# An attention stage written out step by step: which steps carry no output product, where a tile's first output product is issued, and which engine makes the masks

## The chip, the cores and the metric

The kernel runs on one core of a Trainium2 chip. The metric is the device time of one execution in microseconds (us). Before the change the median of three runs is 1140.16 us (1139.94 to 1144.62). Everything is 32-bit floating point (f32) unless a type is named.

## The reference, cut to what matters

A batch of 32 sequences of 32 tokens with 512 features passes four conditional layers, each added to its input. The first three mix tokens and features with weights that are picked per sequence. The fourth, in which the change lies, is grouped-query attention over a paged cache:

```python
q = rope(rmsnorm(x @ Wq.T));  k = rope(rmsnorm(x @ Wk.T));  v = x @ Wv.T   # 32 query heads, 8 key heads, D = 128
kc, vc = k_cache[block_table], v_cache[block_table]       # 16 pages of 32 keys: 512 old keys a sequence
scores = q @ concat(kc, k).T * SCALE                      # 544 keys
scores = where(old key < cache_seqlens | new key, scores, -1e30)
o = softmax(scores) @ concat(vc, v)
x = x + o.reshape(32, 32, 32 * 128) @ Wo.T
```

The 4 query heads of a key head and the 32 tokens of a sequence make the 128 rows of one score matrix, so there are 32 x 8 = 256 score matrices of 128 x 544.

## The kernel before, in words

The first part (up to about 370 us of the profile) does the first three layers and the projections to queries, keys and values, and stores them in DRAM. The second part is the attention stage. It is one loop over steps n = 0 to 263 (`N + LAG`, N = 256, LAG = 8) under a manual schedule: every engine gets its instructions in exactly the order in which the Python code issues them, and synchronisation between engines is added by semaphores. With b, g = divmod(n, 8), step n belongs to sequence b and key head g. One step issues, in this order:

- at g = 0 to 3 one gather of cached values (`load_value_chunk`, line 252, an indirect DMA issued by GpSimd, POOL in the profile), and at several g loads of keys, queries and new values on SyncE's queue (SP);
- `scores(b, g)`: TensorE (PE) multiplies 128 queries by 288 keys (line 1019) and by 256 keys (line 1020) into the one score buffer `s_ps` in PSUM (there is only one, so the scores of the next step wait until it has been read). VectorE (DVE) reads it with one custom instruction (line 1028): it adds `mask`, scales by `rq`, writes `pr` to SBUF and gives each row's extreme in `low` by a short read-accumulator instruction;
- `exponentials`: ScalarE (ACT) takes the exponential of `pr` in place and the row sums (line 1044);
- `flip_kept`: DVE transposes finished outputs `os` into `ot` (line 1154), the step after they are made, with one exception in each four sequences;
- `fill` (n below 37 only): one of four passes of the last value projections (line 312);
- from n = 4 on, `place` for the four steps older probabilities of one quad (4 key heads): DVE transposes blocks of 32 x 32 (`turned`, line 1057), and four copies of 32 partitions x 512 put the pieces where the value product needs them (`placed`): two or three of them by ACT (line 1069), the rest by POOL (line 1071) for the first quad of a sequence (g = 4 to 7) and by DVE (line 1073) for the second (g = 0 to 3); for sequence 0 ACT takes one or two and POOL the rest of both quads. At the first step of a quad POOL gathers the new keys' probabilities (`pq`, line 1080); at the third step, which is every n with n % 4 = 2, PE transposes them (`pn_ps`, line 1084) and ACT copies the result out (line 1086);
- `share(n)`: from n = 37 on, products of the output projection. A tile is 4 sequences (128 tokens x 512 outputs), made of 32 products `f_ps` (line 1174, 128 x 512 each, accumulated in one PSUM buffer of which there is one). A tile's products are spread over 32 steps by the lists `SHARE` and `LAST` (the seventh tile, t = 6): entry i says how many products step n = 37 + 32 t + i issues. `sum` of each list is 32. After a tile's last product DVE adds it to the residual (`x`, line 1183), and that read frees the PSUM buffer. At i = 0 the sum of the tile before is also stored, by a DMA that ACT issues;
- `values` for the step eight before: PE makes four products 128 x 128 (line 1097) from `placed` and the cached values; at the fourth step of the first quad also 8 small products of the new keys (line 1117, `new_values`). At the fourth step of a quad `keep` makes DVE take the reciprocals (line 1131) and scale the output out of PSUM (`os`, line 1133);
- at g = 7 `see_keys(b + 1)`: DVE writes the next sequence's mask, 128 x 544, from a table of 16-bit key numbers and the sequence's length (line 218). There is one mask buffer, which the custom instructions of all eight steps of a sequence read.

In f32 every product is two passes on PE, so the profile counts twice as many (256 x 2 instructions for line 1019).

The lists before are `SHARE`, with entries 0 at i = 16 and i = 24 (steps with g = 5), and `LAST`, with entries 0 at i = 16, 18, 24 and 26 (g = 5, 7, 5, 7). Both have a 2 at i = 2 (g = 7) and i = 8 (g = 5). The end of the program (`finish_by_halves`) makes the eighth tile after the loop.

Of the kernel before, what the change touches and what calls it, by code (L numbers as in the profile page):

```python
# [21 lines left out]
B, S, HID = 32, 32, 512  # L22
D, HQ, HK = 128, 32, 8
# [5 lines left out]
BT = P // S  # L29
# [30 lines left out]
def cond_resid_kernel(  # L60
# [18 lines left out]
    nc = tc.nc  # L79
# [89 lines left out]
    def load_table(b: int):  # L169

        pages_of[b] = const.tile([1, NPP], I32, tag="pages", name=f"pages_{b}", bufs=4)
        at = B + b * NPP
        nc.sync.dma_start(out=pages_of[b], in_=pick[:, at : at + NPP])
# [34 lines left out]
    def load_keys(b: int):  # L208

        pool = homes[b % 2]  # L210
        kt = pool.tile([P, NPP + 1, HK * PSIZE], F32, tag="kt", name=f"kt_{b}")
        kts[b] = kt

    mask = const.tile([P, LT], F32, name="mask")

    def see_keys(b: int):

        nc.vector.tensor_scalar(
            mask, key_i, len_f[:, b : b + 1], 1.0e30, ALU.is_ge, ALU.mult
        )  # L220

    def load_new_keys(b: int):
        nc.sync.dma_start(out=kts[b][:, NPP, :], in_=k_d[b])

    def load_queries(b: int, q: int):

        qts[b, q] = qp.tile([P, HALF * S], F32, tag="qt", name=f"qt_{b}_{q}")
        nc.sync.dma_start(
            out=qts[b, q], in_=q_d[b][:, q * HALF * S : (q + 1) * HALF * S]
        )  # L230

    def load_inverses(b: int):
        rqs[b] = const.tile([P, 2, QUAD], F32, tag="rq", name=f"rq_{b}", bufs=2)
        nc.sync.dma_start(out=rqs[b], in_=r_d[:, b * S : (b + 1) * S])

    def page_keys(b: int):
        return [kts[b][:, n, :] for n in range(NPP)]
# [10 lines left out]
    def load_value_chunk(b: int, c: int):  # L248
        if c == 0:
            vts[b] = homes[b % 2].tile([P, L // P, HK * D], F32, tag="vt", name=f"vt_{b}")  # L250
        at = b * (L // P) + c
        nc.gpsimd.indirect_dma_start(  # L252
            out=vts[b][:, c, :],
            out_offset=None,
            in_=v_cache,
            in_offset=bass.IndirectOffsetOnAxis(ap=v_idx[:, at : at + 1], axis=0),
        )
# [751 lines left out]
    def quad_of(b: int, g: int):  # L1009
        return b, g // QUAD  # L1010

    def scores(b: int, g: int):
        kt, qt = kts[b], qts[quad_of(b, g)]
        kt4 = kt.rearrange("d n (h o) -> d n h o", h=HK)

        ps = ps_s.tile([P, 2 * L], F32, tag="s", name=f"s_ps_{b}_{g}")
        u = g % QUAD
        q = qt[:, u * REP * S : (u + 1) * REP * S]
        nc.tensor.matmul(ps[:, first:L], q, kt4[:, :N_LOW, g, :], start=True, stop=True)  # L1019
        nc.tensor.matmul(  # L1020
            ps[:, L : first + LT], q, kt4[:, N_LOW:, g, :], start=True, stop=True
        )
        if u == 0:
            prs[quad_of(b, g)] = tp.tile([P, QUAD, LT], F32, tag="pr", name=f"pr_{b}_{g}")
        pr = prs[quad_of(b, g)][:, u, :]
        low = tp.tile([P, 1], F32, tag="low", name=f"low_{b}_{g}", bufs=4)

        nc.vector.tensor_tensor_reduce(  # L1028
            pr,
            ps[:, first : first + LT],  # L1030
            mask,
            rqs[b][:, g // QUAD, u : u + 1],
            3.0e38,
            ALU.add,
            ALU.min,
            low,
        )
        return b, g, pr, low

    def exponentials(b: int, g: int, pr, low):  # L1040
        quad, u = quad_of(b, g), g % QUAD
        if u == 0:
            dens[quad] = tp.tile([P, QUAD], F32, tag="den", name=f"den_{b}_{g}", bufs=4)
        nc.scalar.activation(  # L1044
            pr, pr, AF.Exp, bias=low, scale=-1.0, accum_out=dens[quad][:, u : u + 1]
        )
# [114 lines left out]
    def load_residual(t: int):  # L1161
        x3s[t] = tp.tile([P, HID], F32, tag="os", name=f"x3_{t}")
        nc.sync.dma_start(out=x3s[t], in_=x_d[t])

    def finish(t: int, hs):

        for h in hs:
            if h == 0:

                if t < NT - 1:  # L1170
                    pfs[t] = ps_p.tile([P, HID], F32, tag="f", name=f"f_ps_{t}")
                else:
                    pfs[t] = ps_s.tile([P, 2 * L], F32, tag="s", name=f"f_ps_{t}")
            nc.tensor.matmul(  # L1174
                pfs[t][:, :HID],
                ots[t, h // HALF][:, h % HALF, :],
                wo(h),
                start=(h == 0),
                stop=(h == (HQ if t < NT - 1 else HALF) - 1),
            )  # L1180
            if h == HQ - 1:
                x3 = x3s.pop(t)
                nc.vector.tensor_tensor(x3, x3, pfs.pop(t), ALU.add)
                added[t] = x3
# [15 lines left out]
    def store_sum(t: int, eng):  # L1200
        eng.dma_start(out=out[t * P : (t + 1) * P, :], in_=added.pop(t))
# [2 lines left out]

    SHARE = [1, 1, 2, 1, 1, 1, 1, 1, 2, 1, 1, 1, 1, 1] + [1, 1, 0] + [1] * 7 + [0] + [1] * 7

    LAST = SHARE[:14] + [1, 1, 0, 1, 0, 1, 1, 1, 1, 1, 0, 1, 0] + [1, 1, 1, 2, 2]
    BEGIN = BT * HK + LAG - QUAD + 1  # L1210

    def share(n: int):
        t, i = divmod(n - BEGIN, BT * HK)
        if 0 <= t < NT - 1:
            parts = LAST if t == NT - 2 else SHARE
            done = sum(parts[:i])
            finish(t, range(done, done + parts[i]))
        if i == 0 and 0 < t:
            store_sum(t - 1, nc.scalar)

    units = [(b, g) for b in range(B) for g in range(HK)]
    N = len(units)
# [24 lines left out]
    with tc.manual_schedule(engines=order):  # L1247
        for n in range(N + LAG):
            b, g = divmod(n, HK)
            if n == FILLED + 2:  # L1250
                pa.close()
                late = ctx.enter_context(tc.tile_pool(name="b_w", bufs=1))
                places.append(late)
                wos[1] = late.tile([P, LATE, HID], F32, name="wo_1")
            if BEGIN <= n <= N and n % (BT * HK) == 0:

                load_residual((n - BEGIN) // (BT * HK))
            if n < N:
                if g == 0 and b >= 1:
                    load_queries(b, 1)  # L1260
                if g == 0 and 1 <= b < B - 1:
                    load_keys(b + 1)
                    load_new_keys(b + 1)
                    keys.dsts = page_keys(b + 1)
                    keys.transfer(slice(0, 12))
                if g < L // P and b >= 2:
                    load_value_chunk(b, g)
                if g == QUAD and b < B - 1:
                    load_queries(b + 1, 0)
                    load_inverses(b + 1)  # L1270
                    if b >= 1:
                        keys.transfer(slice(12, NPP))
                    if 1 <= b < B - 2:
                        load_table(b + 2)
                if g == QUAD + 1 and b >= 1:
                    load_new_values(b)
                if g == QUAD + 2 and b < B - 2:
                    keys = Picked(nc.sync, k_cache, pages_of.pop(b + 2), range(NPP), K_SHAPE)
                scored = scores(b, g)
                exponentials(*scored)  # L1280
            flip_kept(n)
            fill(n)
            if n in unstored:
                store_values(*unstored.pop(n))
            if n == QUAD + 1:
                load_new_values(0)
            if n in WO_AT:
                load_wo(2 * WO_AT.index(n))
            if QUAD <= n < N + QUAD:
                bq, i = divmod(n - QUAD, HK)  # L1290
                q, j = divmod(i, QUAD)
                if j == 0:
                    gather_new(bq, q)
                if j == 2:
                    flip_new(bq, q)
                place(bq, q, j)
            share(n)
            if n >= LAG:
                values(*units[n - LAG])
            if n < N and g == HK - 1 and b < B - 1:  # L1300
                see_keys(b + 1)
            if n > N + QUAD:
                at = 4 * (n - N - QUAD - 1)
                finish(NT - 1, range(at, at + 4))
        assert not dens and not prs and not pos and not placed and not pns
        load_residual(NT - 1)
        flip_kept(N + LAG)
        finish(NT - 1, range(3 * QUAD, HALF))
        finish_by_halves(NT - 1)
# [76 lines left out]
```

## Time and profile before

| | us |
|---|---|
| median of 3 runs | 1140.16 |
| the profiled execution's own time | 1139.8 |
| its span, first to last instruction | 1138.0 |
| PE busy | 1122.4 (99%) |
| DVE busy | 807.5 (71%) |
| ACT busy | 752.8 (66%) |
| POOL busy | 559.0 (49%) |
| masks of line 218, 32 instructions | 20.5 (DVE) |
| output products of line 1174, 480 passes | 241.3 (PE) |
| additions of line 1183, 7 instructions | 4.6 (DVE) |

"Busy" adds the durations of an engine's instructions without overlap. For PE the ends are modelled, so that a pass that had to wait for its weights looks like a longer pass; a stall is therefore read from the distance between the starts of two passes, and from PEld, the loading of weights, which shows what it waited for. In a timeline each line is: start, duration, engine, line and operation, written tile <- read tiles, shape, count, and in brackets the idle time just before and what ended it. The share of the granted TensorE clock was full over the whole span.

### The profile page before, as it was taken

What the parts mean: (1) busy time and instruction counts of PE and PEld (TensorE: products, weight loads), DVE (VectorE), ACT (ScalarE), POOL (GpSimd) and SP (SyncE); (2) the same over time, 40 slices, a digit from 0 to 9 for tenths busy, and PEclk for the clock granted to TensorE, in tenths of its full rate; (3) what the DMA queues carried; (4) which work ended last, traced back from release to release, by engine and by line L of the source; (5) the groups of instructions that cost most, each with busy time, mean ns of one, the idle gap of its engine ahead of it and who ended that gap; (6) DMA issues with size and microseconds to landing.
All of it is one profiled execution on the core that took longest, in us unless ns stands there. A gap on an engine that the chain in (4) does not pass through costs nothing. (4 is left out here: it accounts for less than half of the span.)

```text
span 1138.0 us, 18994 instructions
## 1 busy us (share of the span) xinstructions
PE 1122.4 (99%) x5432; PEld 730.1 (64%) x5432; DVE 807.5 (71%) x1670; ACT 752.8 (66%) x1900; POOL 559.0 (49%) x719
## 2 busy tenths in 40 slices
PE   8999999999999999999999999999999999999998
PEld 5554444444444577777777777777777777777766
DVE  2510688886977487777778868877877777877851
ACT  1211377576666688777777777877777877777750
POOL 3411689899897544533443344334533443344310
PEclk9999999999999999999999999999999999999999
DMA  8998447688786587888667756765776676766610
GB/s 319 392 419 347 176 133 220 174 234 229 197 232 169 159 272 267 271 308 284 216 217 243 248 190 230 262 229 178 243 251 223 200 239 224 240 202 214 222 29 10
DMA packets 173354, 259.24 MB, mean 228 GB/s; under 512 B 31522, under 2 KB 130466, under 8 KB 168770
## 3 DMA queue, kind: packets, MB, share of 16 engines
q1 hardware_dynamic: 152226, 184.22, 51.0%
q0 software_dynamic: 20016, 71.97, 17.7%
q10 hardware_dynamic: 1008, 1.84, 0.4%
q8 instruction: 44, 0.72, 0.3%
q14 instruction: 60, 0.49, 0.1%
HBM read 228.46 MB, written 37.88 MB: 234 GB/s over the span
## 5 line engine op out<-in xcount | busy, mean ns | idle before, releaser
L1069 ACT COPY placed<-turned 32x512 f32<-32x512 f32 x539 | 332.8, 617 | 31.4 <-DVE turned L1057 24.0
L1097 PEld LDWEIGHTS o_ps<-vt,placed 128*128 128x128 f32 x2048 | 267.0, 191 | 118.5 <-issue 89.4
L1028 DVE CUSTOM_DVE_ANT_0 pr<-s_ps,mask,rq 128x544 f32<-128x544 f32 x256 | 200.6, 784 | 132.5 <-PE s_ps L1020 124.0
L1044 ACT ACTIVATE pr<-pr,low 128x544 f32<-128x544 f32 x256 | 192.2, 751 | 132.7 <-DVE low L1028 130.8
L1071 POOL COPY placed<-turned 32x512 f32<-32x512 f32 x268 | 163.6, 611 | 230.8 <-DVE turned L1057 164.1
L1097 PE MATMUL o_ps<-vt,placed 128*128 128x128 f32 x2048 | 270.4, 275 | 5.6 <-ACT placed L1069 2.8
L1174 PE MATMUL f_ps<-wo,ot 128*128 128x512 f32 x480 | 241.3, 594 | 0.7
L1057 DVE STREAM_TRANSPOSE turned<-pr 128x512 f32<-128x512 f32 x256 | 178.7, 698 | 0.1
L1019 PE MATMUL s_ps<-kt,qt 128*128 128x288 f32 x512 | 174.4, 422 | 1.4 <-DVE low L1028 0.5
L1020 PE MATMUL s_ps<-kt,qt 128*128 128x256 f32 x512 | 152.3, 379 | 0.4 <-issue 0.4
L252 POOL DMA_INDIRECT vt<-in_v_cache_dram,v_idx x128 | 128.0, 1000 | 36.6 <-issue 25.4
L1020 PEld LDWEIGHTS s_ps<-kt,qt 128*128 128x128 f32 x512 | 97.2, 190 | 27.5 <-DMA kt<-in_k_cache_dram 0.8
L434 POOL TENSOR_TENSOR ra<-ra,rs 128x512 f32<-128x512 f32 x80 | 103.9, 1306 | 10.6 <-DVE rs L429 6.4
L1174 PEld LDWEIGHTS f_ps<-wo,ot 128*128 128x128 f32 x480 | 85.8, 190 | 28.6 <-issue 13.9
L1073 DVE COPY placed<-turned 32x512 f32<-32x512 f32 x217 | 94.6, 436 | 5.5
L1080 POOL COPY pq<-pr 128x128 f32<-128x128 f32 x64 | 18.6, 290 | 149.4 <-PE o_ps L1097 94.6
L447 ACT ACTIVATE sq<-x 128x128 f32<-128x128 f32 x256 | 76.4, 302 | 19.3 <-DVE x L405 13.9
L1019 PEld LDWEIGHTS s_ps<-kt,qt 128*128 128x128 f32 x512 | 77.3, 191 | 17.0 <-DVE low L1028 10.6
L544 ACT COPY r<-m 128x512 f32<-128x512 f32 x80 | 46.4, 580 | 52.4 <-PE m L389 51.4
L389 PE MATMUL m<-t_pair,x_sums 128*128 128x512 f32 x160 | 75.3, 593 | 0.6 <-ACT r L544 0.6
L389 PE MATMUL m<-w_pair,x3t 128*128 128x512 f32 x160 | 75.2, 592 | 0.0
L389 PE MATMUL m<-w_pair,x_sums 128*128 128x512 f32 x160 | 72.1, 592 | 0.0
(129 smaller groups left out, 1223.6 us busy)
## 6 DMA issues: line engine op xcount, KB each, us to landing
kt<-in_k_cache_dram SPq DMA_DIRECT2D x512, 128.0 KB
wa<-in_w_adapt_dram SPq DMA_DIRECT2D x32, 1024.0 KB
q_d<-st SPq DMA_DIRECT2D x128, 128.0 KB
qt<-q_d SPq DMA_DIRECT2D x64, 256.0 KB
w_pair<-in_w_qkv_dram SPq DMA_DIRECT2D x20, 512.0 KB
o_d<-in_w_o_dram SPq DMA_DIRECT2D x16, 512.0 KB
wo<-o_d SPq DMA_DIRECT2D x16, 512.0 KB
k_d<-st SPq DMA_DIRECT2D x32, 128.0 KB
```

The source lines that it names most:

```text
L252: nc.gpsimd.indirect_dma_start(out=vts[b][:, c, :], out_offset=None, in_=v_cache, in_offset=bass.IndirectOffsetOnAxis(ap=v_idx[:, at : at ...
L389: nc.tensor.matmul(ps, of[:, k], by[:, k], start=(not more and k == 0), stop=(k == KH - 1), skip_group_check=more,)
L434: nc.gpsimd.tensor_tensor(u.a, u.a, u.s, ALU.add)
L1019: nc.tensor.matmul(ps[:, first:L], q, kt4[:, :N_LOW, g, :], start=True, stop=True)
L1020: nc.tensor.matmul(ps[:, L : first + LT], q, kt4[:, N_LOW:, g, :], start=True, stop=True)
L1028: nc.vector.tensor_tensor_reduce(pr, ps[:, first : first + LT], mask, rqs[b][:, g // QUAD, u : u + 1], 3.0e38, ALU.add, ALU.min, low,)
L1044: nc.scalar.activation(pr, pr, AF.Exp, bias=low, scale=-1.0, accum_out=dens[quad][:, u : u + 1])
L1057: nc.vector.transpose(part, pr)
L1069: nc.scalar.copy(dst, src)
L1071: nc.gpsimd.tensor_copy(dst, src)
L1097: nc.tensor.matmul(po, pt[:, c, :], vt[:, c, g * D : (g + 1) * D], start=(c == 0 and q == 0), stop=(c == L // P - 1 and q == 1),)
L1174: nc.tensor.matmul(pfs[t][:, :HID], ots[t, h // HALF][:, h % HALF, :], wo(h), start=(h == 0), stop=(h == (HQ if t < NT - 1 else HALF) - 1),)
```

## The change

Three edits. The masks of sequences 1 to 31 are made by POOL instead of DVE, and are issued inside step g = 7 right behind its `scores`, no longer at that step's end; the first sequence's mask stays on DVE. The entries 0 of the lists move to i = 17 and 25 (`SHARE`) and to i = 16, 17, 21 and 25 (`LAST`); steps with i = 17, 21 and 25 are ones with n % 4 = 2. At i = 0 of a tile (n = 37, 69, 101 and so on, g = 5) `share` is called behind `values`, elsewhere ahead of it as before.

```diff
-    def see_keys(b: int):
+    def see_keys(b: int, eng=nc.vector):
-        nc.vector.tensor_scalar(
+        eng.tensor_scalar(
             mask, key_i, len_f[:, b : b + 1], 1.0e30, ALU.is_ge, ALU.mult
         )
...
-    SHARE = [1, 1, 2, 1, 1, 1, 1, 1, 2, 1, 1, 1, 1, 1] + [1, 1, 0] + [1] * 7 + [0] + [1] * 7
+    SHARE = [1, 1, 2, 1, 1, 1, 1, 1, 2, 1, 1, 1, 1, 1] + [1] * 3 + [0] + [1] * 7 + [0] + [1] * 6
-    LAST = SHARE[:14] + [1, 1, 0, 1, 0, 1, 1, 1, 1, 1, 0, 1, 0] + [1, 1, 1, 2, 2]
+    LAST = SHARE[:14] + [1, 1, 0, 0, 1, 1, 1, 0, 1, 1, 1, 0, 1] + [1, 1, 1, 2, 2]
...
                 scored = scores(b, g)
+                if g == HK - 1 and b < B - 1:
+                    see_keys(b + 1, nc.gpsimd)
                 exponentials(*scored)
...
-            share(n)
+            begins = (n - BEGIN) % (BT * HK) == 0
+            if not begins:
+                share(n)
             if n >= LAG:
                 values(*units[n - LAG])
-            if n < N and g == HK - 1 and b < B - 1:
-                see_keys(b + 1)
+            if begins:
+                share(n)
```

## The prediction

> **What bounds the kernel now.** I read the page's busy times first, then the list of waits, then the timeline at the three places that the change touches. From the page:
>
> ```profile
> PE 1122.4 (99%) x5432; PEld 730.1 (64%) x5432; DVE 807.5 (71%) x1670; ACT 752.8 (66%) x1900; POOL 559.0 (49%) x719
> ```
>
> PE is the bound, and the change takes no product away from it. All it can win is time in which PE is held up, which hides in the starts of its passes. The list of waits (us in total, times, longest) names what holds its weight loads:
>
> ```profile
> PEld o_ps L1097 <- POOL placed L1071: 14.1, 24, 2.1
> PEld o_ps L1097 <- ACT placed L1069: 11.0, 30, 1.4
> PEld s_ps L1019 <- DVE low L1028: 10.6, 27, 1.4
> PEld f_ps L1174 <- DVE x L1183: 3.1, 6, 0.5
> ```
>
> Not all of that is lost, since weights load beside the pass before. So I measured PE's loss itself: start of a pass to start of the next, less the same distance where nothing waits. Undisturbed, scores take 0.92 us, an output product 0.86, four value products 0.90, PE's transpose 0.11. A full step is 2.67 us, one without a product 1.81. When a weight load is held until the data are there, the next pass also shows its 0.10 of loading, so a wait costs its length beyond the free start plus 0.10.
>
> **Part 1, a tile's first product behind the values.** Timeline at step 69, the second tile's first:
>
> ```profile
> 561.30 0.59 PE L1020 MATMUL s_ps<-kt,qt 128*128 128x256 f32 x2
> 561.31 0.65 DVE L1183 TENSOR_TENSOR x<-x,f_ps 128x512 f32<-128x512 f32 x1
> 562.01 0.30 PEld L1174 LDWEIGHTS f_ps<-wo,ot 128*128 128x128 f32 x2 [0.52 <-DVE x L1183]
> 562.02 1.13 PE L1174 MATMUL f_ps<-wo,ot 128*128 128x512 f32 x2
> ```
>
> The product starts 0.72 after line 1020, elsewhere 0.44 (570.66 to 571.10), and takes 1.13 instead of 1.02: 0.39 lost, at six beginnings (tiles 1 to 6): 2.3 us. Behind the values the product comes 0.90 later, at about 562.6, while the addition ends at 561.96: the stall goes, and the values, whose quad was placed at least a step before (g = 5), take its place. What is late next is DVE's custom instruction of the step, which the next scores need; a full step covers it. The store that ACT issues keeps its place on ACT's queue, because values at g = 5 issue nothing there; SP's order does not change at all. Gain 2.3.
>
> **Part 2, the empty steps.** Step 53 (no product) and the scores of 54:
>
> ```profile
> 515.88 0.65 PE L1019 MATMUL s_ps<-kt,qt 128*128 128x288 f32 x2
> 517.00 0.78 DVE L1028 CUSTOM_DVE_ANT_0 pr<-s_ps,mask,rq 128x544 f32<-128x544 f32 x1 [0.55 <-PE s_ps L1020]
> 517.84 0.30 PEld L1019 LDWEIGHTS s_ps<-kt,qt 128*128 128x128 f32 x2 [0.19 <-DVE low L1028]
> 517.84 0.75 PE L1019 MATMUL s_ps<-kt,qt 128*128 128x288 f32 x2
> ```
>
> A loop through DVE (scores, custom, next scores) lasts 1.96, then 0.10 of loading, against 1.81 of PE work: 0.26 lost after each empty step. With the transpose inside, PE's own work is 1.92, and 0.15 is lost. DVE has no copies at g = 6, as at g = 5, so the loop is no longer. Gain 0.11 for each of the 12 empty steps of tiles 0 to 5: 1.3 us. The price lies on ACT: the transposing step gives it one more copy (line 1086, 0.24), and shortening exactly that step makes its exponential of the next step about 0.2 later and with it its copies for the first value product of the next sequence. By the rows (exponential 0.75, copies 1.25, from the starts of steps 117 to 119) those copies are there 6.41 after the start of the empty step, and PE's weights must load by about 6.41: no slack. I charge 0.3 us over all tiles, bounds 0 and 0.15 x 14 = 2.1.
>
> The seventh tile (`LAST`) by the same measure loses 3.1 before: 0.26, 0.26, 0.28 and 0.26 at the scores of 246, 248, 250 and 254, 0.31 at the values of 248 (ACT's copies), 0.10 at 249, and 1.59 at step 256, where no scores are left to cover ACT's copies. After it I expect 0.26 behind step 245, 0.15 behind 246, 250 and 254, and 0.9 at 256: a product now stands in step 255 (0.86 of cover), less the 0.2 by which ACT is late. That is 1.6; gain 1.5.
>
> **Part 3, the masks.** Steps 119 (g = 7) to 122:
>
> ```profile
> 704.69 0.78 DVE L1028 CUSTOM_DVE_ANT_0 pr<-s_ps,mask,rq 128x544 f32<-128x544 f32 x1 [1.37 <-PE s_ps L1020]
> 706.17 1.27 POOL L1071 COPY placed<-turned 32x512 f32<-32x512 f32 x2 [1.52 <-DVE rden L1131]
> 706.44 0.69 DVE L1133 TENSOR_TENSOR os<-o_ps,rden 128x512 f32<-128x512 f32 x1 [0.28 <-PE o_ps L1097]
> 707.05 0.69 DVE L218 TENSOR_SCALAR mask<-key_i,len_f 128x544 f32<-128x544 int16 x1
> 707.87 0.78 DVE L1028 CUSTOM_DVE_ANT_0 pr<-s_ps,mask,rq 128x544 f32<-128x544 f32 x1
> 708.02 1.05 PE L1097 MATMUL o_ps<-vt,placed 128*128 128x128 f32 x8
> 710.82 0.78 DVE L1028 CUSTOM_DVE_ANT_0 pr<-s_ps,mask,rq 128x544 f32<-128x544 f32 x1
> 711.67 0.75 PE L1019 MATMUL s_ps<-kt,qt 128*128 128x288 f32 x2
> ```
>
> The mask and the 0.13 behind it hold DVE for 0.82. The custom instruction of step 120 starts at 707.87 instead of 1.12 after its scores (706.24), 707.36; behind it wait the transposes of `os` and `pr` and two copies, so that of step 121 is at 710.82 instead of 710.03, and the scores of 122 come 0.09 late and show 0.10 of loading. The longer first scores pass (0.75 instead of 0.65) marks eleven such steps with g = 2 in tiles 0 to 5, 2.1 us together; ahead of n = 37 steps 27 and 35 lose 0.41 each, of which 0.15 is the empty step's own. With DVE rid of 0.82 the customs start 0.5 and more earlier, which covers all of it. Gain 2.1 and 0.5.
>
> On POOL the mask waits for the custom of g = 7, which read the old mask (ends 705.47). Behind it on POOL are the two copies that started at 706.17, then the value gathers, then `pq`. The copies' end must be seen by PE about 0.10 before 708.02: they must start by 706.53, so a mask that starts at 705.53 and is followed after 0.04 may last 1.00 us at no cost. DVE needs it only at 707.36. Its gathers stay put: the first of them was at 707.71, and their values are used a sequence later. Longer than 1.00, the mask delays the value products of about 20 sequences (27 masks are made from step 39 on, and in 7 of those steps two products give slack) by the excess plus 0.10.
>
> No such instruction of POOL is in this trace. Nearest rows, from the groups and the start of the timeline:
>
> ```profile
> L1071 POOL COPY placed<-turned 32x512 f32<-32x512 f32 x268 | 163.6, 611 | 230.8 <-DVE turned L1057 164.1
> L434 POOL TENSOR_TENSOR ra<-ra,rs 128x512 f32<-128x512 f32 x80 | 103.9, 1306 | 10.6 <-DVE rs L429 6.4
> 8.33 0.58 POOL L143 IOTA key_i<- 128x512 int16 x1
> 1.57 0.28 POOL masks.py:199 TENSOR_SCALAR_AFFINE_SELECT ident<-ident 128x128 f32<-128x128 f32 x1
> ```
>
> One input and 512 elements cost 0.61, so 544 about 0.64; writing 512 16-bit numbers 0.58, so 0.62 is the lower end. The upper end is two inputs, 1.31 for 512, so 1.38 for 544. The select compares each element, as the mask does, and takes 0.28 for 128 elements, as much as a plain copy of that size (line 1080, 290 ns). I take 0.7, at no cost, and keep 1.38: 20 x (0.38 + 0.10) = 9.6. One place pays anyway: at step 8 PE waits for POOL (393.45, 1.15 <- POOL placed), so the mask in step 7 costs its length, about 0.6, once.
>
> The Trainium skill speaks against this edit: its GPSIMD Engine Reference, section Elementwise — side-by-side cycle accounting, keeps elementwise work on VectorE and measures a two-input addition 1.96 times slower on GpSimd. This trace agrees for two inputs (1306 ns of line 434 against 686 of DVE's line 419, 1.9 times). By that ratio the fastest mask here, 464 ns, would be an estimated 0.91 us, still within the slack, and the sum would be the same.
>
> **The sum.** 2.3 + 1.3 + 1.5 + 2.1 + 0.5 = 7.7, less 0.3 (ACT) and 0.6 (step 8): 6.8 us. The profiled execution took 1139.8 (span 1138.0, 1.8 around it), 0.4 below the median: 1133.0 against it, 1133.4 against the median. I say 1133.3.
>
> **Rivals.**
> - GpSimd becomes the late one: the mask is priced like two inputs (1.38). For it: a scalar per row, two operations and a conversion in one instruction, none of which POOL does elsewhere here. Against: the select's row. Time: 1133.3 + 9.6 + 0.7 at step 8 = 1143.6, slower than before. It costs from 1.00 on, and turns the gain into a loss at about 1.2 (20 x 0.33 = 6.6 at 1.23). Past 1.5 the kernel is slower by over 0.5%. Chance 0.17, of it 0.11 for past 1.5.
> - ACT takes the empty step's place: its copies are late by 0.1 to 0.2 behind every transposing empty step. For: no slack by my count, 30 waits on ACT in the list. Against: of those few moved a pass. 14 x 0.15 to 0.25 is 2.1 to 3.5 instead of 0.3: about 1136. Chance 0.15.
> - The edit on masks does not do what it says: another DVE instruction keeps the scores of g = 2 late. Then 2.6 less: 1136. Against: 0.82 is removed where 0.2 is missing. Chance 0.08.
> - My forecast: 0.60, its own range 1131.3 to 1135.5.
>
> **How the numbers follow.** About 0.5% (5.7 us) is what a measurement of this kernel can tell from no change: the line is at 1134.5, close to my sum. Of the forecast's 0.60 I put 0.50 below it and 0.10 above; with 0.02 of the others that is 0.52 faster. The other 0.37 is the same: 0.10 + 0.13 + 0.08 and 0.06 of a mask between 1.00 and 1.5. Slower: 0.11. The range 1131.3 to 1142 leaves out some 0.05 below and 0.13 above, and takes in a mask up to about 1.3.
>
> **What would show it.** Right: line 218 on POOL at 0.6 to 1.0; no wait of PEld L1174 for DVE x; waits of L1019 for DVE low behind i = 17 and 25 that cost 0.15; first scores passes of 0.65 at g = 2. Wrong: line 218 above 1.00 with PEld o_ps waiting on POOL at g = 0; or the same waits on ACT.

## The result, and the profile after

The changed kernel takes 1165.40 us (median of 5 runs, 1163.58 to 1166.18) against 1139.98 (median of 5, 1139.40 to 1144.62): 1.0221 times as long, 95% interval 1.0208 to 1.0233. It is 25 us slower where 7 us of gain were forecast. The profiled execution took 1165.8 us, its span is 1164.0.

From the page: the busy times, and the group of the mask.

```profile
PE 1125.6 (97%) x5432; PEld 729.6 (63%) x5432; DVE 786.6 (68%) x1639; ACT 751.2 (65%) x1900; POOL 625.4 (54%) x750
L218 POOL TENSOR_SCALAR mask<-key_i,len_f 128x544 f32<-128x544 int16 x31 | 65.2, 2104 | 18.8 <-DVE low L1028 18.7
```

The span grew by 26.0 and PE's busy time by only 3.2: the other 22.8 are open idle time of PE, whereas its losses before hid in the starts of its passes. DVE lost about as much as the 31 masks had cost it (807.5 to 786.6), and POOL gained 66: one mask takes 2.10 us there, against 0.46 to 0.86 on DVE (0.64 on average) and against the 0.7 of the forecast. The list of waits says who pays:

```profile
PEld o_ps L1097 <- POOL placed L1071: 51.8, 31, 3.1
PE o_ps L1097 <- POOL placed L1071: 26.8, 24, 2.3
PEld o_ps L1097 <- ACT placed L1069: 11.1, 30, 1.4
PEld s_ps L1019 <- DVE low L1028: 7.1, 10, 1.4
```

The second line stood at 0.3 us, once, before: now PE itself stands still 24 times for POOL's copies. The line `PEld f_ps L1174 <- DVE x L1183` of before has gone, ACT's line has not moved (11.0 before), and the scores wait 10 times for DVE instead of 27. So three of the four lines that the prediction shows behave as it said, and the one of POOL's copies does not. The timeline from step 118 (without a product, with the transpose) over 119 (g = 7) to 122:

```profile
717.16 0.75 PE L1019 MATMUL s_ps<-kt,qt 128*128 128x288 f32 x2
718.38 0.78 DVE L1028 CUSTOM_DVE_ANT_0 pr<-s_ps,mask,rq 128x544 f32<-128x544 f32 x1 [0.65 <-PE s_ps L1020]
719.35 2.10 POOL L218 TENSOR_SCALAR mask<-key_i,len_f 128x544 f32<-128x544 int16 x1 [0.29 <-DVE low L1028]
721.48 0.78 DVE L1028 CUSTOM_DVE_ANT_0 pr<-s_ps,mask,rq 128x544 f32<-128x544 f32 x1 [0.66 <-POOL mask L218]
721.51 1.26 POOL L1071 COPY placed<-turned 32x512 f32<-32x512 f32 x2
722.83 1.16 PE L1097 MATMUL o_ps<-vt,placed 128*128 128x128 f32 x8 [0.95 <-POOL placed L1071]
726.49 0.65 PE L1019 MATMUL s_ps<-kt,qt 128*128 128x288 f32 x2
```

Read it from the mask. It starts 0.19 after the custom instruction that read the old mask has ended (0.06 in the forecast) and lasts until 721.45. The two copies follow at once, take as long as before (1.26 and 1.27) and end at 722.77, and the value passes start 0.06 later; PE stood still for 0.95, and the first pass is 0.10 longer. The custom instruction of step 120 waited for the mask too, but by less. The two outer lines are the gains: the scores behind the empty step show only the 0.10 of loading (0.75 for 0.65), and those of g = 2 show nothing any more. At step 69, a tile's first, the stall has gone as well:

```profile
570.87 0.65 DVE L1183 TENSOR_TENSOR x<-x,f_ps 128x512 f32<-128x512 f32 x1
571.29 1.05 PE L1097 MATMUL o_ps<-vt,placed 128*128 128x128 f32 x8
572.18 1.02 PE L1174 MATMUL f_ps<-wo,ot 128*128 128x512 f32 x2
```

Where the time went, by the prediction's own measure (distances between starts of passes, less the undisturbed ones), over steps 0 to 263, in us (the numbers are rounded one by one):

| place | before | after | difference |
|---|---|---|---|
| g = 0 from step 40 on, values wait for POOL: 20 sequences x 1.22, 7 x 0.36 | 0 | 26.9 | +26.9 |
| steps 16, 24, 32 | 3.1 | 6.2 | +3.1 |
| step 8, values wait for POOL | 0.5 | 2.4 | +1.9 |
| steps 8 and 9, a dip of PE's clock (told at the end) | 0 | 1.7 | +1.7 |
| tile beginnings | 2.3 | 0 | -2.3 |
| empty steps and the rest of the seventh tile | | | -2.6 |
| g = 2 from step 42 on, step 250 with them | 2.4 | 0 | -2.4 |
| steps 26, 27, 34 and 35 | 1.1 | 0.3 | -0.8 |
| step 56: one load of keys came late, in this execution of before only | 1.1 | 0 | -1.1 |

The sum is +24.4. Another 1.1 of the 26.0 lies ahead of the stage, which the change does not touch (PE's first scores start at 374.6 instead of 373.5). About 0.5 is not assigned.

### The profile page after: what moved, and what is told of

It reads as the page before. It is cut to its first block, busy times and chain, and to the rows that moved or that the text cites. A ratio compares the mean times of both kernels' runs of the same rounds, so it can differ in the third digit from the quotient of the medians.

```text
span 1164.0 us, 18995 instructions
## 1 busy us (share of the span) xinstructions
PE 1125.6 (97%) x5432; PEld 729.6 (63%) x5432; DVE 786.6 (68%) x1639; ACT 751.2 (65%) x1900; POOL 625.4 (54%) x750
## 4 chain that ended last, share of the span: by engine, by line
PE 78%; POOL 8%; issue 8%; DVE 3%; DMA 2%; ACT 1%; SPq 0%; POOLq 0%; DVEq 0%
PE o_ps L1097 18%; PE f_ps L1174 14%; PE m L389 12%; PE s_ps L1019 10%; PE s_ps L1020 8%; PE qkv L312 4%; POOL placed L1071 3%; PE adapt L747 2%; PE base L722 2%; POOL ra L434 2%; PE o_ps L1117 2%; POOL rs L429 1%; POOL mask L218 1%; PE f_ps L1194 1%; PE f_ps_last L1194 1%
## 5 line engine op out<-in xcount | busy, mean ns | idle before, releaser
L1097 PE MATMUL o_ps<-vt,placed 128*128 128x128 f32 x2048 | 274.1, 277 | 29.5 <-POOL placed L1071 26.8
L1174 PE MATMUL f_ps<-wo,ot 128*128 128x512 f32 x480 | 240.6, 593 | 0.0
L1174 PEld LDWEIGHTS f_ps<-wo,ot 128*128 128x128 f32 x480 | 86.9, 190 | 25.1 <-issue 13.9
L1073 DVE COPY placed<-turned 32x512 f32<-32x512 f32 x217 | 91.2, 420 | 5.5
L1080 POOL COPY pq<-pr 128x128 f32<-128x128 f32 x64 | 21.9, 343 | 126.1 <-PE o_ps L1097 74.5
L218 POOL TENSOR_SCALAR mask<-key_i,len_f 128x544 f32<-128x544 int16 x31 | 65.2, 2104 | 18.8 <-DVE low L1028 18.7
```

Of the source, the lines that this page charges most:

```text
L1097: nc.tensor.matmul(po, pt[:, c, :], vt[:, c, g * D : (g + 1) * D], start=(c == 0 and q == 0), stop=(c == L // P - 1 and q == 1),)
L1174: nc.tensor.matmul(pfs[t][:, :HID], ots[t, h // HALF][:, h % HALF, :], wo(h), start=(h == 0), stop=(h == (HQ if t < NT - 1 else HALF) - 1),)
```

## The experiments

My theory after the result: only the price of the mask on POOL was wrong, and everything else in the sum holds. Rivals: the new lists cost something too (ACT's copies are late behind each transposing empty step); POOL's copies run longer beside DVE's work that now lies elsewhere; or it is where the mask stands, not what it costs. The second needs no run: POOL's 268 copies take 608 ns each on average, 611 before.

**Masks back on DVE, the rest of the change kept (e1_masks_back).**

```diff
 scored = scores(b, g)
-if g == HK - 1 and b < B - 1:
-    see_keys(b + 1, nc.gpsimd)
...
+if n < N and g == HK - 1 and b < B - 1:
+    see_keys(b + 1)          # at the step's end, on DVE
```

> The changed kernel with the masks back on VectorE at the end of step g = 7; the order at a tile's start and the lists stay changed. Theory A (only the mask's 2.10 us on GpSimd, against 1.00 us of slack, turned the result): the other two parts give what was worked out, 2.3 + 1.3 + 1.5 - 0.3 = 4.8 us, so 1135.2 against 1140.0, and the timeline shows 0.15 lost behind steps i = 17 and 25 and the old 0.19 at g = 2. Theory B (the empty steps or the order at a tile's start cost time too): 1139 or more.

Measured: 1134.77 (1134.43 to 1135.13) against 1139.41, ratio 0.9958 [0.9945, 0.9972]. The value passes lose nothing at g = 0 from step 40 on; the stalls at g = 2 are back (2.4 us by the start-to-start count). So the two other edits together are a gain of 4.6, and the whole loss comes with the mask.

**The masks alone (e2_masks_only).** The kernel before with nothing but this:

```diff
+if g == HK - 1 and b < B - 1:
+    see_keys(b + 1, nc.gpsimd)          # behind scores(b, g)
...
-if n < N and g == HK - 1 and b < B - 1:
-    see_keys(b + 1)
```

> The kernel before with nothing but the masks moved to GpSimd, at the place that the change gives them. Theory A: all of the loss and 4.8 us more, since the gains of the other two parts are missing: 1165.4 + 4.8 = 1170. Theory B: the masks explain only a part, so 1145 to 1160.

Measured: 1169.91 (1168.34 to 1170.59) against 1139.41, ratio 1.0267 [1.0253, 1.0281]. The mask takes 2100 ns here too, beside the old lists. The edit by itself costs 30.5; the other two bring 4.6 with the masks on DVE (e1) and 4.5 with them on POOL (1169.91 less 1165.40, from different series of runs). The edits add up.

**The tile's first product alone (e5_start_only).** The kernel before with `begins` and the moved `share` only.

```diff
+begins = (n - BEGIN) % (BT * HK) == 0
+if not begins:
+    share(n)
 if n >= LAG:
     values(*units[n - LAG])
+if begins:
+    share(n)
```

> The kernel before with nothing but a tile's first output product behind the values of its step. Forecast by the prediction's part 1: 0.39 at six starts, 2.3 us less, 1137.1 against 1139.4; no wait of a weight load of line 1174 for VectorE's addition. If DVE's lateness only moves on to the next scores: no difference.

Measured: 1136.84 (1136.18 to 1138.00) against 1139.29, ratio 0.9980 [0.9971, 0.9989]: -2.45 for a forecast of -2.3. The six losses, 2.27 by the count, are 0.

**The lists alone (e6_lists_only).** The kernel before with the new `SHARE` and `LAST` only.

```diff
-SHARE = [...] + [1, 1, 0] + [1] * 7 + [0] + [1] * 7
+SHARE = [...] + [1] * 3 + [0] + [1] * 7 + [0] + [1] * 6
...
-LAST = SHARE[:14] + [1, 1, 0, 1, 0, 1, 1, 1, 1, 1, 0, 1, 0] + [1, 1, 1, 2, 2]
+LAST = SHARE[:14] + [1, 1, 0, 0, 1, 1, 1, 0, 1, 1, 1, 0, 1] + [1, 1, 1, 2, 2]
```

> The kernel before with nothing but the two new lists. Forecast by part 2: 1.3 + 1.5 - 0.3 = 2.5 us less, 1136.9 against 1139.4. If ACT is late behind the transposing empty steps (rival 2): 1138.5 to 1140.

Measured: 1137.13 (1136.47 to 1137.84) against 1139.29, ratio 0.9981 [0.9972, 0.9990]: -2.16 for a forecast of -2.5. An ordinary empty step now loses 0.145, as worked out. At i = 19 and 27 of tiles 0 to 5, where ACT's later copies would hold the values, the count shows no loss. The rival on ACT has fallen. This gain and that of e5 make 4.6, what e1 has with both.

**What is dear in the mask (e4_probe_forms, e10_probe_pairs).** At the end of the kernel before, POOL runs single instructions on a table of 512 numbers, with nothing else queued on it. The arguments of the main ones:

```diff
+nc.gpsimd.tensor_scalar(made, ki, one, 1.0e30, ALU.is_ge, ALU.mult)     # the mask's form, from 16 bits
+nc.gpsimd.tensor_scalar(made, kf, one, 1.0e30, ALU.is_ge, ALU.mult)     # from f32
+nc.gpsimd.tensor_scalar(made, kf, one, None, ALU.is_ge)
+nc.gpsimd.tensor_scalar(made, kf, one, 1.0e30, ALU.add, ALU.mult)
...
+nc.gpsimd.tensor_scalar(made, kf, one, 2.0, ALU.subtract, ALU.mult)     # second probe
+nc.gpsimd.tensor_scalar(made, kf, one, 2.0, ALU.mult, ALU.mult)
+nc.gpsimd.tensor_scalar(made, kf, one, None, ALU.mult)
```

> The kernel before, and behind its last copies on GpSimd, where that engine has no more work, nine instructions with 512 elements a row (one with 256) into a tile that nothing reads, to price the mask's form: a copy from 16-bit integers; the mask's form; the same from 32-bit floats; with one operation; with a constant instead of a scalar per row, two operations and one; addition and multiplication by a scalar per row; addition of a constant; the mask's form with 256. Theory: the fixed part is small and 544 elements cost 2.10, so the mask's form takes about 2.0 with 512 and 1.1 with 256. If the conversion is what costs, the form from floats falls to about 0.7; if the scalar per row, the forms with constants do; if the second operation, the forms with one do; if every tensor_scalar on this engine costs that, none does.

> The kernel before with eight more instructions of 512 elements of 32-bit floats on GpSimd behind its last copies, into a tile that nothing reads: an addition and a multiplication by a scalar per row and a constant, the same by two constants, a multiplication and an addition, a subtraction and a multiplication, two multiplications, a subtraction and a maximum, a comparison and an addition, one multiplication. If the comparison is what is dear, all the arithmetic pairs take about 0.7 and the comparison 2.0; but one addition alone took 1.50, so if only chosen pairs have a fast way, just the first ones take 0.7 and the others 1.5 to 2.0.

Measured, instruction by instruction in the traces (the kernels themselves took 1138.93 and 1139.57, one run each). First probe: the mask's form from 16 bits, the same from f32, the comparison alone, addition and multiplication.

```profile
L1309 POOL TENSOR_SCALAR probe_made<-key_i,len_f x1: 2010/2010/2010, 1100.2 to 1100.2; 128x512 f32<-128x512 int16 x1
L1310 POOL TENSOR_SCALAR probe_made<-probe_keys,len_f x1: 1995/1995/1995, 1102.3 to 1102.3; 128x512 f32<-128x512 f32 x1
L1311 POOL TENSOR_SCALAR probe_made<-probe_keys,len_f x1: 1568/1568/1568, 1104.4 to 1104.4; 128x512 f32<-128x512 f32 x1
L1314 POOL TENSOR_SCALAR probe_made<-probe_keys,len_f x1: 691/691/691, 1109.6 to 1109.6; 128x512 f32<-128x512 f32 x1
```

Second probe: subtraction with multiplication, two multiplications, one multiplication.

```profile
L1312 POOL TENSOR_SCALAR probe_made<-probe_keys,len_f x1: 2015/2015/2015, 1103.2 to 1103.2; 128x512 f32<-128x512 f32 x1
L1313 POOL TENSOR_SCALAR probe_made<-probe_keys,len_f x1: 697/697/697, 1105.3 to 1105.3; 128x512 f32<-128x512 f32 x1
L1316 POOL TENSOR_SCALAR probe_made<-probe_keys,len_f x1: 1578/1578/1578, 1110.3 to 1110.3; 128x512 f32<-128x512 f32 x1
```

The durations can be believed: each next instruction starts about 0.1 after the end of the one before (1102.3, 1104.4). Neither the 16-bit source nor the scalar per row is what is dear (a constant instead of the scalar: 1926). The pair of operations is: comparison and multiplication 2.0, addition and multiplication 0.7. The forecast of 0.7 was the right price for another pair. Nor do the surroundings in the kernel make the mask dear: its form costs as much alone, with POOL idle otherwise.

**The cheap pair in place of the mask's (e8_cheap_form).** The changed kernel with a pair of operations that POOL does quickly; it leaves out the masking of keys, so only its time is of use.

```diff
-mask, key_i, len_f[:, b : b + 1], 1.0e30, ALU.is_ge, ALU.mult
+mask, key_i, len_f[:, b : b + 1], 1.0e-30, ALU.add, ALU.mult
```

> The changed kernel with an addition and a multiplication by 1e-30 in place of the comparison and the multiplication by 1e30 in every mask (no key is masked out). Alone on GpSimd this form took 0.69 us for 512 elements, so about 0.73 for 544: under the slack of 1.00, at the same place in the queue. Theory A: the prediction's sum holds as it stands, 6.8 us less than before, 1132.5 to 1133.5 against 1139.3, with 0.6 to 0.7 lost at step 8 alone. If it is the place and not the length that costs: over 1145.

Measured: 1132.35 (five runs from 1132.08 to 1133.13, a sixth of 1139.23) against 1139.23, ratio 0.9951 [0.9933, 0.9969].

```profile
L218 POOL TENSOR_SCALAR mask<-key_i,len_f x31: 717/717/721, 391.9 to 1062.4; 128x544 f32<-128x544 int16 x31
```

This run is the prediction's assumption made true: an instruction at the same place on POOL, of the same shapes, that lasts 0.72. The time is 1.0 below the 1133.3 forecast. No value pass at g = 0 loses anything from step 40 on, and step 8 loses 0.5 more than before, for which 0.6 was charged.

**Half a mask (e9_half_mask).** The changed kernel, whose masks made by POOL cover 272 keys only (the other half stays as made for the first sequence, so again only the time is of use).

```diff
+w = LT if b == 0 else LT // 2
-mask, key_i, len_f[:, b : b + 1], 1.0e30, ALU.is_ge, ALU.mult
+mask[:, :w], key_i[:, :w], len_f[:, b : b + 1], 1.0e30, ALU.is_ge, ALU.mult
```

> The changed kernel with masks of 272 instead of 544 keys from the second sequence on (the other half stays as the first sequence's). By the two widths measured, 1.15 us for 256 and 2.01 for 512, it lasts 1.21. Theory A (a cost of the excess over 1.00 plus 0.10, at 20 sequences, and the length less 0.7 more at step 8): 1132.7 + 20 x 0.31 + 0.5 = 1139.4, as long as before. If the slack is larger, 1133 to 1136; if the cost does not go with the length, 1150 or more.

Measured: 1139.24 (1138.36 to 1139.89) against 1139.23, ratio 1.0000 [0.9991, 1.0008]. The timeline at the same place (the edit adds a line, so line numbers are one higher):

```profile
706.76 1.19 POOL L219 TENSOR_SCALAR mask<-key_i,len_f 128x272 f32<-128x272 int16 x1 [0.29 <-DVE low L1029]
709.32 0.97 PEld L1098 LDWEIGHTS o_ps<-vt,placed 128*128 128x128 f32 x8 [0.87 <-POOL placed L1072]
```

At 1.19 us each of the 20 sequences loses 0.306. The prediction's formula, excess over 1.00 plus 0.10, gives 0.29; at 2.10 it gives 1.20, and 1.22 was found; at 0.72 it gives nothing, and nothing was found. All three agree with the formula. This one lies on the break-even, which the prediction put at about 1.2.

**Another place for the same instruction (e3_masks_pool_early, e7_masks_dve_early).** With two mask buffers the mask need not wait for the last read of the old one. Two 16-bit buffers take the bytes of one f32 buffer. In e3 POOL makes the mask half a sequence earlier, at g = 3; in e7 DVE makes it at the end of step g = 6.

```diff
-mask = const.tile([P, LT], F32, name="mask")
+masks = [const.tile([P, LT], mybir.dt.bfloat16, name=f"mask_{i}") for i in range(2)]
...
+if g == QUAD - 1 and b < B - 1:             # e3, ahead of scores(b, g)
+    see_keys(b + 1, nc.gpsimd)
...
+if n < N and g == HK - 2 and b < B - 1:     # e7, at the step's end
+    see_keys(b + 1)
```

> The changed kernel with two mask buffers of 16-bit floats (the same bytes as one of 32 bits), and GpSimd makes the next sequence's mask at step g = 3, where it waits for over 5 us in the trace of before. Theory A (the place, between the last reader and the copies of step g = 7, made the mask dear): no value product waits for GpSimd any more, all three parts gain, 1133 to 1134. Theory C (a mask on GpSimd costs wherever it stands, by holding VectorE's or its own queue up): over 1138.

> The changed kernel with the two 16-bit mask buffers, and VectorE makes the next mask at the end of step g = 6, where it waits 1.4 us for the scores of g = 7. Theory A: the stalls at g = 2 go as well when VectorE is only rid of the mask behind the scaling of the outputs: 1133 to 1134, within 1 us of the early masks on GpSimd. If the stalls at g = 2 had another cause, it stays with the kernel that has the masks back at step g = 7, at 1135.

Measured against 1139.41: e3 1133.02 (1132.67 to 1133.69), ratio 0.9944 [0.9930, 0.9957]; e7 1131.40 (1130.98 to 1133.63), ratio 0.9936 [0.9923, 0.9950]. The mask in each:

```profile
L218 POOL TENSOR_SCALAR mask<-key_i,len_f x31: 2101/2133/2308, 37.1 to 1050.0; 128x544 bf16<-128x544 int16 x31
L218 DVE TENSOR_SCALAR mask<-key_i,len_f x32: 318/320/360, 36.3 to 1059.6; 128x544 bf16<-128x544 int16 x32
```

In e3 the instruction still takes 2.1 us and costs almost nothing, because nothing that PE needs soon is queued behind it. So the loss needs both: the price and the place. In e7 the mask lies ahead of the scores of g = 7, for which DVE waits 1.37 at step 119 of the kernel before, and takes 0.32. The 16 bits help there: the first sequence's mask, made on DVE in both kernels, takes 0.36 in e7 and 0.51 before. The stalls at g = 2 have gone without POOL. e7 is the best version measured, faster than both kernels. Its lead over e3 is 1.6 by the medians. The two profiled executions differ by 2.7: steps 0 to 36 take 1.35 less (95.12 against 96.47), where POOL's copies are late already; 1.1 lies ahead of the stage, where the traces here differ by up to 1.2 anyway, and 0.3 behind step 36.

## Why the prediction was wrong

- **What bounds the kernel: right.** PE's own work did not change; the time is decided by what holds its passes, and the start-to-start distances show it.
- **Part 1: right.** Forecast 2.3, measured 2.27 in the trace and 2.45 as a run by itself.
- **Part 2: right.** 0.26 behind an empty step became 0.145 (0.15 forecast). At the end of the seventh tile 0.91 was found (0.9 forecast), and 0.15 at each of the three places for which 0.15 was forecast. The 0.3 charged to ACT was not found. As a run by itself the part brought 2.16; the sum had 2.5.
- **Part 3, gain on DVE: right.** The eleven stalls at g = 2 (2.1 in the trace, 2.1 forecast) went, and so did 0.8 at steps 26 to 35 (0.5 forecast); the twelfth, 0.28 at step 250, the prediction has in part 2. That rival has fallen too.
- **Part 3, price on POOL: the step that failed.** It reads "I take 0.7, at no cost", with 0.62 and 1.38 as its ends. The instruction takes 2.10. The lower rows were a copy and a writing of numbers, the upper one an addition of two inputs, and I treated two inputs as the worst that one pass over 544 elements could cost. That end was not an end: no row of the trace showed POOL comparing and multiplying by scalars in one instruction, and I noted that ("none of which POOL does elsewhere here") and still let known rows close the range above. The row that weighed most, the affine select of 0.28 for 128 elements, compares too, but it is another instruction; the mask's form costs 1.15 us for 256 elements. The estimate of 0.91, from the Trainium skill's ratio for an addition, failed in the same way: POOL's mask at 2.10 is 4.5 times DVE's fastest of 0.46 and 3.3 times its mean of 0.64.
- **What a longer mask does: right.** The slack of 1.00, the 20 sequences, the excess plus 0.10 and the break-even of 1.2 all held (e9, e8). With 2.10 the formula gives 20 x 1.20 = 24.0 for the 20 sequences; 24.4 were found. The slack itself came out well partly by luck. Its own terms (copies of 1.27 that end about 0.10 ahead of 708.02, 0.04 behind the mask) give 1.08, not 1.00; in the run the mask starts 0.13 later than reckoned, and the passes start only 0.06 behind the copies. By the losses of e9 and of the changed kernel the slack is 0.99. For the seven with two products the formula gives 2.10 less 1.86 (the slack and one product more) plus 0.10, 0.34 each; 0.36 were found.
- **Left out of the sum:** the masks of steps 15, 23 and 31. Only step 7 was charged. At 0.72 that is right (e8: 3.06 us lost at steps 16, 24 and 32, as before); at 2.10 these three cost 3.1.
- **Rival 1** named this mechanism, with its place and the point from which it decides, and had the wrong size: 9.6 instead of 26.9, for the same reason. Its chance beyond 1.5 us, 0.11, was what should have been larger, with an upper end that no neighbouring row could give.

## What to carry to other kernels

When an operation moves to another engine and the trace has no row of that very operation there, its two operations included, the dearest neighbour is no upper bound: give the estimate an open end, work out from which duration it decides, and time the instruction by itself first. An engine that is busy half of the time still has places where its queue is on the path: ask what stands behind the new instruction, how soon TensorE needs that, and whether a second buffer lets the instruction stand elsewhere. Here the best version measured left the mask on DVE, one step earlier and in half the bytes.

## What the runs showed of the hardware that was not expected

GpSimd's instruction with scalars has very different prices by its operations. For 128 x 512 f32, pairs made of additions and multiplications only took 0.62 to 0.70 us, and every pair tried with a subtraction or a comparison took 1.93 to 2.02. A single operation is dearer than a quick pair: 1.49 to 1.58, be it a comparison, an addition or a multiplication. For the mask's form, 2010 ns for 512 elements and 1152 for 256 give 3.35 ns an element and 0.29 fixed; 544 elements would then take 2.12, and 2.10 was measured. Why the single operation is dear, no run tells.

In the changed kernel's profile, PE's idle 2.25 us at step 8 (394.26 to 396.51) was followed by 3.4 us at half the full clock. The stretches of the span, with busy time and instructions of PE, PEld, DVE, ACT and POOL, then the granted clock, DMA share and GB/s:

```profile
396.50:397.00 0.50, 0.49 (x2) 0.49 (x3) 0.00 (x0) 0.49 (x2) 0.42 (x2) 0.64 0.71 209
398.00:399.00 1.00, 1.00 (x5) 0.86 (x4) 0.00 (x0) 0.00 (x0) 0.13 (x1) 0.50 0.71 171
400.00:400.50 0.50, 0.50 (x2) 0.20 (x2) 0.21 (x1) 0.00 (x0) 0.00 (x0) 0.95 0.88 299
```

The means of the two outer stretches put the halved clock between about 396.64 and 400.05, 3.41 us. Eight value passes took 1.99 us there instead of 1.05, and 1.7 us were lost. With the masks alone (e2) PE was idle for 2.24 at the same place, and the clock stayed at 1.00. So an idle time of this length can be followed by such a dip, and need not be. The Trainium skill (TensorE: Matmul & The Clock Gate, section Part 1: The HAM clock gate) says that activity is judged in windows of 3413 ns that run on regardless of the kernel, and that the clock is halved after an idle window of that length. The length of the dip agrees. The length of the idle time does not: 2.25 was enough once, and in the 3.41 us ahead of the drop PE had been busy for 1.16.

The twelve traces tell more than these two stalls. In each, cut the time into stretches of 3.413 us, the length of the dip, so that one ends where the clock drops (in every trace it drops once behind PE's last pass, and in the changed kernel once more, at 396.64). The 13 stretches that end in a drop hold 0 to 1.23 us of PE's busy time; no other stretch holds less than 1.49. PE's idle 2.25 in the changed kernel fell whole into one stretch (393.23 to 396.64). With the masks alone an edge at 394.13 split the 2.24 (393.80 to 396.04), and the stretch behind it still held 1.49. In these traces, then, what goes with the dip is how little PE works in one such stretch, not how long the idle time is; no run shifts a stall on purpose to test it.
